# A two-layer graph network on one core: the loads of adj's own columns moved from ScalarE's queue to SyncE's, and the last block's product in three PSUM banks

## The chip, the core and the metric

The kernel runs on one core of a Trainium2 chip, all in float32. The metric is the device time of one launch in microseconds (us). Engines are named as in the profile: PE (TensorE), DVE (VectorE), ACT (ScalarE), POOL (GpSimd) and SP (SyncE). SP computes nothing here; it issues transfers.

## The reference, cut to what matters

`adj` is 3327 x 3327, sparse, with all of the diagonal set and the first nodes' rows and columns by far the fullest. `x` is 3327 x 512. The kernel gets both padded to 3328 rows, 26 blocks of 128, and adj transposed (`adjT`). The hidden width is 128.

```python
h = relu(layernorm(x))
x = x + adj @ (relu(adj @ (h @ W1) + b1) @ W2) + b2        # layer 0

h = relu(layernorm(x))                                     # layer 1
a, b = adj @ h, adj @ h                                    # the same sum twice
attn_a = sigmoid([a, h] @ Wa.T + ba)
attn_b = sigmoid([b, h] @ Wb.T + bb)
hs = h @ W_sa
s_left, s_right = hs @ a_sa[0, :512], hs @ a_sa[0, 512:]
e = where(adj != 0, exp(-leaky_relu(s_left[:, None] + s_right[None, :], 0.01)), 0)
x_a = (e / (e.sum(1) + 1e-5)) @ hs
x_b = adj @ (h @ W_gcnb) + b_gcnb
x = x + sigmoid(attn_a * x_a + attn_b * x_b)
```

## The kernel before, in words

The work has three parts.

**The first pass over adj** (from L593) computes the hidden layer of layer 0 and, at the same time, finds out where adj is not zero. It takes adjT's columns in seven chunks, listed in `back`: six of 512 columns and a last one of 256. I call them passes 0 to 6. In each pass `load_adj` (L295) brings adjT in tiles of two row blocks, 512 KB, through SP's queue, into six buffers (`adjp`). TensorE accumulates `acc_u` over the 26 row blocks j (L622), and DVE reduces each tile to `most`, the largest value of each group of 32 columns (L629). After a pass `make_g` turns its result: `gT`, a relu on ACT (L390), then four transposes into `pg` on PE (L393), a copy on DVE and a store through ACT's queue.

From `most` of one pass, `make_lists` makes, during the next pass, the lists of the groups that are not empty: small steps on PE (`p_off`, `p_sh`, `p_list`, L517 to L567) and on DVE (`at` and others, L482 to L591). By those lists POOL gathers the groups of adj (L180) into the buffers `ae[i]`, one for each block i, which part 3 uses.

Pass 0 has more to do. For each row block j it also loads block j+4 of x (L356, SP's queue, five buffers), normalizes block j+3 on DVE and ACT (`normalize`: `scaled` is its statistics' scale), transposes block j+2 (`pt`, L372) and makes `u` of block j+1 (`pu`, L380). During pass 0 POOL writes constants and clears the 25 buffers `ae[1]` to `ae[25]` one after another (L479). An `ae` buffer must be cleared before anything is loaded into it.

In two kinds of blocks a part of `ae[i]` isn't gathered by a list but loaded at a known place. The 18 blocks in `OWN` get their own columns on the diagonal. The 8 of them in `TOP` also get the columns of the first 64 nodes. This is `load_own` (L210): for each such part and each half of the block's 128 nodes one transfer of 16 KB, 52 in all. They go through ACT's queue. `load_behind` (L335) issues them from pass 2 on at j = 6, 10, 16, 19 and 22, one block each time, and each is tied by `pace` to the `acc_u` matmul of that j. `load_behind` also loads, through ACT's queue, the columns of the first 128 nodes (`a_hub`) in five parts, and pieces of `W_sa` and `W2`. After pass 3 ACT's queue gets `b2_row`.

**The second pass over adj** (L916 to L968) makes layer 0's output, normalizes it and makes layer 1's rows. It reads x again: the first such loads, into buffers called `xb` (L704), are free to go as early as their buffers allow.

**The block loop** (L1278 to L1330) treats the blocks of layer 1: `attend` (scores and exponentials), `sums` (the sums over gathered rows, L1135), `turn` (transposes) and `weigh` (the products with the weights): `p_b` (L1189) and `p_a` (L1197), each in PSUM banks of 128 x 512. `finish` (L1004) joins the two, and per column piece scales `p_a` on ACT, adds on DVE, takes a tanh on ACT, adds x on DVE and stores. For the last block, L1330, the columns go in two pieces, 0 to 257 and 257 to 512 (`WH` is 257), both in one bank; other blocks have one piece.

A scheduler sets the order of the instructions on each engine from the dependencies and the order in the source. `queued(...)` places an instruction behind another one of its own engine's work, `pace` adds a wait. An engine works through its instructions in order, and a queue's waits hold up what stands behind them on the same engine. `psA` and `psB` are two pools of four PSUM banks each.

Of the kernel before, what the change touches and what calls it, by code (L numbers as in the profile page):

```python
# [10 lines left out]
AF = mybir.ActivationFunctionType  # L11
# [7 lines left out]
P = 128  # L19
# [3 lines left out]
HALF = P // 2  # L23
# [32 lines left out]
OWN = TOP + (1, 6, 7, 8, 12, 13, 14, 15, 17, 18)  # L56
# [10 lines left out]
def kernel(  # L67
# [17 lines left out]
    nc = tc.nc  # L85
    NP, D = x.shape
# [4 lines left out]
    back = [(c0, CW) for c0 in range(NP - CW, NP % CW - 1, -CW)]  # L91
# [19 lines left out]
    psA = ctx.enter_context(tc.tile_pool(name="psA", bufs=4, space=bass.MemoryType.PSUM))  # L111
    psB = ctx.enter_context(tc.tile_pool(name="psB", bufs=4, space=bass.MemoryType.PSUM))

    def bank(pool, name):
        return pool.tile([P, CW], F32, tag="bank", name=name)
# [91 lines left out]
                            row_a[:, f : f + 1], NP * NG - 1,  # L207
                        )

    def load_own(i, load):  # L210

        n = segments(i)[0][1]
        for k in range(extra[i]):
            for h in range(2):
                cols = slice(i * P + h * HALF, i * P + (h + 1) * HALF)
                rows = slice(0, HALF) if k else cols
                load(
                    ae[i][h * HALF : (h + 1) * HALF, k : k + n + 1 : n, :GW],
                    adjT[rows, cols].rearrange("j (q i) -> j q i", i=GW),
                )  # L220

    columns = gather_adj()

# [62 lines left out]
    with (  # L286
# [38 lines left out]
        def load_weights(k, load):  # L325
# [2 lines left out]
            elif k == KD:  # L328
                load(W2_sb, W2)

        own_order = iter([
            i for c0, w in back for i in range(c0 // P, (c0 + w) // P) if i in OWN
        ])

        def load_behind(added, n, j):  # L335

            def load(out, in_):
                pace(nc.scalar.dma_start(out, in_), added)

            if j == 3 and n <= HUB_LOADS:  # L340
                load_hub(n - 1, load)
            if j == 13:
                load_weights(n - 1, load)
            if n > 1 and j in (6, 10, 16, 19, 22):
                for i in own_order:
                    load_own(i, load)
                    break

        g = {}

# [252 lines left out]
        for n, c in enumerate(back):  # L603
            c0, w = c
# [44 lines left out]
                    nc.scalar.dma_start(b2_row, b2.partition_broadcast(P))  # L649
            lists = make_lists(n, most)  # L650
            next(lists)
        assert next(own_order, None) is None


        for s in range(2):
# [348 lines left out]
    def finish(pool, i, p_a, p_b, esum, cuts=(0, D)):  # L1004

        x1 = pool.tile([P, D], F32, tag="x1", name=f"x1b_{i}")
        nc.sync.dma_start(x1, x1_dram[i])

        f = pool.tile([P, 3], F32, tag="f", name=f"f_{i}")
        nc.vector.tensor_scalar(f[:, 0:1], esum, SUM_EPS, None, op0=ALU.add)  # L1010
        nc.vector.tensor_tensor(f[:, 1:3], p_b[1][:, WH - 2 : WH], node[i][:, 1:3], ALU.add)
        nc.vector.tensor_scalar(f[:, 1:3], f[:, 1:3], LEAST_LOGIT, None, op0=ALU.max)
        nc.scalar.activation(f[:, 1:3], f[:, 1:3], AF.Exp, scale=-1.0)
        nc.vector.tensor_scalar(f[:, 1:3], f[:, 1:3], 1.0, None, op0=ALU.add)
        r = pool.tile([P, 3], F32, tag="r", name=f"r_{i}")
        nc.vector.reciprocal(r, f)
        nc.vector.tensor_tensor(f[:, 0:1], r[:, 0:1], r[:, 1:2], ALU.mult)
        vb = pool.tile([P, D], F32, tag="vb", name=f"vb_{i}")
        nc.vector.tensor_tensor(vb[:, WH:], p_b[1][:, : D - WH], bg_row[:, WH:], ALU.add)
        read_b = nc.vector.tensor_tensor(vb[:, :WH], p_b[0][:, :WH], bg_row[:, :WH], ALU.add)  # L1020
        va = pool.tile([P, D], F32, tag="va", name=f"va_{i}")
        for c0, c1 in zip(cuts, cuts[1:]):
            a, b = va[:, c0:c1], vb[:, c0:c1]
            read_a = nc.scalar.activation(a, p_a[:, c0:c1], AF.Copy, scale=f[:, 0:1])
            nc.vector.scalar_tensor_tensor(b, b, r[:, 2:3], a, op0=ALU.mult, op1=ALU.add)

            nc.scalar.activation(a, b, AF.Tanh, scale=0.5)
            nc.vector.scalar_tensor_tensor(a, a, 0.5, x1[:, c0:c1], op0=ALU.mult, op1=ALU.add)
            nc.sync.dma_start(out[i * P : (i + 1) * P, c0:c1], a)
        return read_a, read_b  # L1030

    with tc.tile_pool(name="spw", bufs=2) as spw:
# [147 lines left out]
        def weigh(i, tyT, es, cuts=(0, D), sums_first=False, between=None):  # L1180


            p_b = [bank(psB, f"p_b_{i}_{k}") for k in range(2)]
            p_s = p_b[1][:, CW - 1 : CW]
            if sums_first:
                add_up(i, es, p_s)
            for n in (1, 0):
                for k in range(KD):
                    last = nc.tensor.matmul(  # L1189
                        p_b[n][:, :WH], tyT[:, k, 0, :], W_g_sb[:, k, n * WH : (n + 1) * WH],  # L1190
                        start=(k == 0), stop=(k == KD - 1),
                    )
            p_a = bank(psB, f"p_a_{i}")
            with queued(between(last) if between else None):
                for c0, c1 in zip(cuts, cuts[1:]):
                    for k in range(KD):
                        last = nc.tensor.matmul(  # L1197
                            p_a[:, c0:c1], tyT[:, k, 1, :], W_sa_sb[:, k, c0:c1],
                            start=(k == 0), stop=(k == KD - 1),
                        )  # L1200
# [126 lines left out]
            for seg in segs[1:]:  # L1327
                sums(1, seg)
        ty, _ = copy_out(1, taken[1]["acc"], True)
        weigh(1, turn(1, ty, True)[0], taken[1]["es"], (0, WH, D), True)[2]()  # L1330

    over = nc.values_load(overflow[0:1, 0:1], min_val=0, max_val=1)
    with tc.If(over > 0):
# [54 lines left out]
        with (  # L1388
# [25 lines left out]
            for c in range(len(chunks)):  # L1414
# [34 lines left out]
                for b in range(w // P):  # L1449
                    i = c0 // P + b  # L1450
                    cols = slice(b * P, (b + 1) * P)
                    p_s = bank(psB, f"q_s_{i}")
                    nc.tensor.matmul(p_s[:, 0:1], esum[:, cols], ones, start=True, stop=True)
                    p_a = bank(psB, f"q_a_{i}")
                    p_b = [bank(psB, f"q_b_{i}_{k}") for k in range(2)]
                    for t, f0, f1, p in (
                        (yT, None, None, p_a),
                        (tT, 0, WH, p_b[0]),
                        (tT, WH, 2 * WH, p_b[1]),
                    ):  # L1460
                        for k in range(KD):
                            w_sb = W_sa_sb[:, k, :] if f0 is None else W_g_sb[:, k, f0:f1]
                            nc.tensor.matmul(
                                p if f0 is None else p[:, :WH], t[:, k, cols], w_sb,
                                start=(k == 0), stop=(k == KD - 1),
                            )
                    finish(l1w, i, p_a, p_b, p_s[:, 0:1])


# [44 lines left out]
```

## Time and profile before

| | |
|---|---|
| median of 3 runs | 716.57 us (715.82 to 716.97) |
| the profiled execution | 805.4 us |
| its span, first to last instruction | 803.6 us |
| PE busy in the span | 722.7 us, 90% |
| ACT busy | 204.7 us, 25% |
| DVE busy | 485.9 us, 60% |
| POOL busy | 456.3 us, 57% |
| bytes moved | 180.47 MB, mean 225 GB/s |
| end of the passes 0 to 6 (start of the relu `gT`) | 64.98, 89.40, 126.63, 158.59, 185.55, 218.26, 236.36 us |

The profiled execution is 89 us longer than the runs' median, so a duration read from the profile is that of this one execution. Idle time of an engine that isn't the bottleneck costs nothing by itself. In rows of groups, the columns are: line, engine, operation, output and inputs, shapes, count; then busy us and mean ns of one; then idle time before, and what ended most of it. In timelines a row is one instruction or a row of like ones: start, duration, engine, line, operation, count, and in brackets the idle time before it with its releaser. SPq, ACTq are the issuing queues of SP and ACT, in time of the issue and not of the transfer.

### The profile page before, as it was taken

What the parts mean: (1) busy time and instruction counts of PE and PEld (TensorE: products, weight loads), DVE (VectorE), ACT (ScalarE), POOL (GpSimd) and SP (SyncE); (2) the same over time, 40 slices, a digit from 0 to 9 for tenths busy, and PEclk for the clock granted to TensorE, in tenths of its full rate; (3) what the DMA queues carried; (4) which work ended last, traced back from release to release, by engine and by line L of the source; (5) the groups of instructions that cost most, each with busy time, mean ns of one, the idle gap of its engine ahead of it and who ended that gap; (6) DMA issues with size and microseconds to landing.
All of it is one profiled execution on the core that took longest, in us unless ns stands there. A gap on an engine that the chain in (4) does not pass through costs nothing.

```text
span 803.6 us, 11919 instructions
## 1 busy us (share of the span) xinstructions
PE 722.7 (90%) x3715; PEld 392.2 (49%) x3715; DVE 485.9 (60%) x1530; ACT 204.7 (25%) x492; POOL 456.3 (57%) x487
## 2 busy tenths in 40 slices
PE   9999959898789889888896399799999999999994
PEld 7775424343364334444443155345555555555553
DVE  6778949789871326555382177347557456575642
ACT  7870000000000324444270123123123113132311
POOL 2300657566667777667607666776767766675400
PEclk9999979899999999997998799999999899999998
DMA  8789959799869999974258566756666766887410
GB/s 277 250 297 307 300 156 297 235 307 290 253 209 292 360 356 331 334 242 139 66 175 306 149 175 201 226 161 179 212 193 195 206 193 195 246 233 223 136 51 31
DMA packets 105738, 180.47 MB, mean 225 GB/s; under 512 B 21217, under 2 KB 38017, under 8 KB 105666
## 3 DMA queue, kind: packets, MB, share of 16 engines
q1 hardware_dynamic: 63632, 111.91, 41.6%
q0 software_dynamic: 22112, 54.46, 24.2%
q10 hardware_dynamic: 19922, 13.25, 5.3%
q8 instruction: 31, 0.51, 0.3%
q14 instruction: 41, 0.34, 0.1%
HBM read 157.64 MB, written 22.26 MB: 224 GB/s over the span
## 4 chain that ended last, share of the span: by engine, by line
PE 71%; issue 11%; DMA 4%; DVE 4%; POOL 4%; another core or an unknown queue 2%; ACT 2%; SPq 0%; POOLq 0%; ACTq 0%; DVEq 0%
PE acc_u L622 18%; PE acc L1135 10%; PE p_b L1189 9%; PE acc_g L925 9%; PE p_a L1197 8%; PE acc_hub L775 3%; PE pu L380 3%; PE px L723 3%; PE ptt L1149 2%; PE acc_s L882 2%; DMA a<-in_adjT_dram 2%; POOL ae L180 2%; POOL hr L180 1%; PE pt L372 1%
## 5 line engine op out<-in xcount | busy, mean ns | idle before, releaser
L180 POOL DMA_INDIRECT ae<-in_adjT_dram,row_a x178 | 184.0, 1034 | 139.1 <-PE acc_u L622 83.5
L622 PE MATMUL acc_u<-a,rows 128*128 128x512 f32 (+1 forms) x364 | 161.7, 583 | 5.1 <-issue 5.1
L180 POOL DMA_INDIRECT hr<-h_rows,row_h x114 | 120.5, 1057 | 55.5 <-issue 27.4
L1189 PE MATMUL p_b<-W_g_sb,tyT 128*128 128x257 f32 x416 | 103.3, 400 | 9.5 <-issue 8.7
L629 DVE TENSOR_REDUCE most<-a 128x32 f32<-128x1024 f32 (+1 forms) x104 | 103.8, 1009 | 11.6 <-DMA a<-in_adjT_dram 9.0
L180 POOL DMA_INDIRECT rows<-h_rows,row_h x64 | 67.6, 1056 | 58.6 <-DVE es_hub L830 20.8
L1189 PEld LDWEIGHTS p_b<-W_g_sb,tyT 128*128 128x128 f32 x416 | 79.6, 196 | 42.7 <-issue 18.2
L622 PEld LDWEIGHTS acc_u<-a,rows 128*128 128x128 f32 x364 | 67.8, 197 | 64.7 <-issue 61.3
L1197 PE MATMUL p_a<-W_sa_sb,tyT 128*128 128x512 f32 (+2 forms) x216 | 95.6, 583 | 2.9 <-issue 2.4
L180 POOL DMA_INDIRECT g_row<-g_rows,row_h x68 | 71.7, 1055 | 30.1 <-issue 16.0
L925 PE MATMUL acc_g<-a,g 128*128 128x512 f32 (+1 forms) x208 | 84.4, 547 | 2.6 <-issue 2.6
L1164 DVE COPY tyT<-ptt 128x512 f32<-128x512 f32 x51 | 35.0, 686 | 75.7 <-PE ptt L1149 35.6
L1135 PE MATMUL acc<-hr,ae 64*64 64x512 f32 x456 | 59.1, 593 | 2.9 <-issue 2.9
L1197 PEld LDWEIGHTS p_a<-W_sa_sb,tyT 128*128 128x128 f32 x216 | 41.2, 191 | 42.0 <-issue 40.1
L925 PEld LDWEIGHTS acc_g<-a,g 128*128 128x128 f32 x208 | 38.6, 191 | 40.3 <-issue 39.2
L727 DVE SCALAR_TENSOR_TENSOR xb<-px,xb 128x512 f32<-128x512 f32 x26 | 17.9, 689 | 58.0 <-PE px L723 26.1
L390 ACT ACTIVATE gT<-acc_u,b_col 128x512 f32<-128x512 f32 (+1 forms) x7 | 4.6, 657 | 168.7 <-DMA ae<-in_adjT_dram 67.8
L988 DVE SCALAR_TENSOR_TENSOR a_hub<-h_own,w_own 128x512 f32<-128x512 f32 x52 | 35.5, 683 | 9.6 <-DMA rows<-h_rows,row_h 9.5
L1071 ACT COPY s_left<-pl 64x64 f32<-64x64 f32 x42 | 8.7, 207 | 124.0 <-PE pl L1067 71.9
L1135 PEld LDWEIGHTS acc<-hr,ae 64*64 64x64 f32 x456 | 19.9, 133 | 35.3 <-issue 34.1
L268 ACT ACTIVATE rows<-xb,ln_b 128x512 f32<-128x512 f32 x26 | 18.8, 722 | 54.2 <-DVE xb L727 24.7
L1135 PE MATMUL acc<-rows,ae 64*64 64x512 f32 x256 | 32.1, 592 | 0.3 <-issue 0.3
(166 smaller groups left out, 979.5 us busy)
## 6 DMA issues: line engine op xcount, KB each, us to landing
a<-in_adjT_dram SPq DMA_DIRECT2D x129, 512.0 KB
h_rows<-rows SPq DMA_DIRECT2D x26, 260.0 KB
h_own<-h_rows SPq DMA_DIRECT2D x26, 260.0 KB
x<-in_x_dram SPq DMA_DIRECT2D x26, 256.0 KB
xb<-in_x_dram SPq DMA_DIRECT2D x26, 256.0 KB
x<-xb ACTq DMA_DIRECT2D x26, 256.0 KB
x1b<-x SPq DMA_DIRECT2D x26, 256.0 KB
out_dram<-va SPq DMA_DIRECT2D x25, 256.0 KB
```

The source lines that it names most:

```text
L180: return nc.gpsimd.indirect_dma_start(out=dst, out_offset=None, in_=table, in_offset=bass.IndirectOffsetOnAxis(ap=rows, axis=0), bounds_ch ...
L380: nc.tensor.matmul(pu[:, :HID], hT[:, k, :], W1_sb[:, k, :], start=(k == 0), stop=(k == KD - 1))
L622: added = nc.tensor.matmul(acc[:, :w], u[j], a[:, :w], start=(j == 0), stop=(j == NB - 1))
L629: nc.vector.tensor_reduce(most[:, : w // GW, j : j + both], tiles.rearrange("p k (b i) -> p b k i", i=GW), axis=AX.X, op=ALU.max, apply_ab ...
L723: on_pe[0] = last_row[2] = nc.tensor.matmul(px, sTs.pop(i), W2_sb, start=True, stop=True)
L775: return nc.tensor.matmul(acc_hub[k], s, made_row(i)[:, :D], start=(n == 0), stop=(n == NB - 1))
L925: on_pe[0] = nc.tensor.matmul(acc[:, :w], g[j], a[:, n % per, :], start=(n == 0), stop=(n == NB - 1))
L988: nc.vector.scalar_tensor_tensor(junk, h[:, :D], 1.0, w_own[:, s, :], op0=ALU.mult, op1=ALU.mult, accum_out=node[i][:, 1 + s : 2 + s],)
L1135: added = nc.tensor.matmul(taken[i]["acc"][h][q * HALF : (q + 1) * HALF, :], both[half_p, q * n + k, :], taken[i][k0][k][half_p, q, :D], s ...
L1164: last = nc.vector.tensor_copy(dst, src)
L1189: last = nc.tensor.matmul(p_b[n][:, :WH], tyT[:, k, 0, :], W_g_sb[:, k, n * WH : (n + 1) * WH], start=(k == 0), stop=(k == KD - 1),)
L1197: last = nc.tensor.matmul(p_a[:, c0:c1], tyT[:, k, 1, :], W_sa_sb[:, k, c0:c1], start=(k == 0), stop=(k == KD - 1),)
```

## The change

`load_own` becomes a generator that issues one of its transfers at each step, on SP's queue. `own_loads` strings the generators of the 18 blocks together. `load_behind` takes one step at each odd j of every pass after the first, whatever is left is issued after the last pass, and the loads are no longer tied to a matmul. In `weigh` the product `p_a` becomes a list of banks, one for each column piece, and `finish` reads each piece from its own bank. The last block has three pieces: 0 to 257, 257 to 448 and 448 to 512 (`HALF` is 64). For all other blocks it stays one piece in one bank of `psB`.

```diff
-    def load_own(i, load):
+    def load_own(i):
 
         n = segments(i)[0][1]
         for k in range(extra[i]):
             for h in range(2):
                 cols = slice(i * P + h * HALF, i * P + (h + 1) * HALF)
-                rows = slice(0, HALF) if k else cols
-                load(
+                rows = slice((k - 1) * HALF, k * HALF) if k else cols
+                nc.sync.dma_start(
                     ae[i][h * HALF : (h + 1) * HALF, k : k + n + 1 : n, :GW],
                     adjT[rows, cols].rearrange("j (q i) -> j q i", i=GW),
                 )
+                yield
...
-        own_order = iter([
-            i for c0, w in back for i in range(c0 // P, (c0 + w) // P) if i in OWN
-        ])
+        own_loads = iter(
+            None
+            for c0, w in back
+            for i in range(c0 // P, (c0 + w) // P)
+            if i in OWN
+            for _ in load_own(i)
+        )
...
             if j == 13:
                 load_weights(n - 1, load)
-            if n > 1 and j in (6, 10, 16, 19, 22):
-                for i in own_order:
-                    load_own(i, load)
-                    break
+            if j % 2:
+                next(own_loads, None)
...
-        assert next(own_order, None) is None
+        for _ in own_loads:
+            pass
...
-        for c0, c1 in zip(cuts, cuts[1:]):
+        for p, c0, c1 in zip(p_a, cuts, cuts[1:]):
             a, b = va[:, c0:c1], vb[:, c0:c1]
-            read_a = nc.scalar.activation(a, p_a[:, c0:c1], AF.Copy, scale=f[:, 0:1])
+            read_a = nc.scalar.activation(a, p[:, : c1 - c0], AF.Copy, scale=f[:, 0:1])
...
-            p_a = bank(psB, f"p_a_{i}")
+            p_a = [bank(psA if n else psB, f"p_a_{i}_{n}") for n in range(len(cuts) - 1)]
             with queued(between(last) if between else None):
-                for c0, c1 in zip(cuts, cuts[1:]):
+                for p, c0, c1 in zip(p_a, cuts, cuts[1:]):
                     for k in range(KD):
                         last = nc.tensor.matmul(
-                            p_a[:, c0:c1], tyT[:, k, 1, :], W_sa_sb[:, k, c0:c1],
+                            p[:, : c1 - c0], tyT[:, k, 1, :], W_sa_sb[:, k, c0:c1],
...
-        weigh(1, turn(1, ty, True)[0], taken[1]["es"], (0, WH, D), True)[2]()
+        weigh(1, turn(1, ty, True)[0], taken[1]["es"], (0, WH, D - HALF, D), True)[2]()
```

More of the change, by code (lines that the diff above doesn't have):

```diff
@@ L1466 @@
                             )
-                    finish(l1w, i, p_a, p_b, p_s[:, 0:1])
+                    finish(l1w, i, [p_a], p_b, p_s[:, 0:1])
 def kernel(**inputs):
```

## The prediction

> **What bounds the kernel now.** I read the page's totals and its chain of waits first, then the groups that the edit touches, then the first pass over adj cut at the seven `gT` activations (one ends each pass), then the timelines of SP, POOL, ACT and PE at the places the edit moves things.
>
> ```profile
> PE 722.7 (90%) x3715; PEld 392.2 (49%) x3715; DVE 485.9 (60%) x1530; ACT 204.7 (25%) x492; POOL 456.3 (57%) x487
> PE 71%; issue 11%; DMA 4%; DVE 4%; POOL 4%; another core or an unknown queue 2%; ACT 2%; SPq 0%; POOLq 0%; ACTq 0%; DVEq 0%
> L622 PE MATMUL acc_u<-a,rows 128*128 128x512 f32 (+1 forms) x364 | 161.7, 583 | 5.1 <-issue 5.1
> L390 ACT ACTIVATE gT<-acc_u,b_col 128x512 f32<-128x512 f32 (+1 forms) x7 | 4.6, 657 | 168.7 <-DMA ae<-in_adjT_dram 67.8
> ```
>
> TensorE carries the chain (71%), the first pass's `acc_u` most of all. DMA is 4% of the chain, SP's and ACT's queues 0%: to the sum, loads are hidden, so a change of who issues them acts only where one holds back PE. The last row shows such a place: before `gT`, which PE's next transposes need, ACT is mostly busy with `ae` loads. The passes, from the busy time in windows (columns: PE, PEld, DVE, ACT, POOL, clock, DMA share, GB/s):
>
> ```profile
> 16.00:40.50 24.50, 24.50 (x158) 18.54 (x157) 19.91 (x66) 19.76 (x45) 11.79 (x57) 1.00 0.78 254
> 64.98:89.40 24.42, 24.42 (x104) 11.01 (x103) 21.62 (x48) 0.69 (x1) 4.07 (x4) 1.00 0.93 303
> 158.59:185.55 26.96, 26.15 (x109) 11.63 (x107) 23.77 (x53) 0.69 (x2) 18.42 (x19) 1.00 0.98 310
> 185.55:218.26 32.71, 25.98 (x141) 12.23 (x141) 30.28 (x69) 0.69 (x1) 21.66 (x21) 1.00 0.89 273
> ```
>
> In pass 0 (the first 24.5 us of it) and pass 1 PE has no gap. Pass 1, 24.42 us, is the length of a pass that nothing holds up. Pass 4 is longer, with DMA at 0.98, and pass 5 longer still. So what costs in pass 0 is paid in full, and what frees pass 4 or 5 is gained.
>
> **The change, part by part.** The sum stands against the profiled execution, 805.4 us (span 803.6, 1.8 around it). The runs' median is 716.57: 88.8 below, about the chain's 11% of "issue" (88 us). I take the edit's differences over unscaled. A measurement of this kernel tells 0.2%, 1.43 us, from no change: faster is below 715.1, slower above 718.0.
>
> *1. What moves.* 52 loads of 16 KB leave ACT's queue, 18 blocks in passes 2 to 5, and go to SP's. The source spreads them over passes 1 to 4 (odd j, 13 a pass). They are no longer tied to a matmul, though, and the compiled order of the changed kernel shows where the scheduler puts them: 22 of 52 in pass 0, between x loads and tiles, the rest in passes 1 to 3, about one a tile, the last ahead of pass 4's second tile. On ACT one costs 0.6 to 0.7 us of issue; on SP an x load 0.33, a tile 0.43, so 0.6 is my value there too (0.33 to 0.7). Their data is small: the 7168 packets of 128 B take 13 ns each, eight an engine, 0.1 us a load. The order moves a second thing: SP's five loads of `xb` (256 KB each, 54 to 60 us, end of pass 0) go into pass 4 and the start of pass 5.
>
> *2. Pass 0: a cost.* The first own load in SP's order is of block 3 and the next of block 24; each waits until POOL has cleared that `ae` buffer, and x loads and tiles stand behind it in SP's order.
>
> ```profile
> 16.80 2.41 SPq L356 DMA_DIRECT2D x<-in_x_dram  x2
> 19.26 0.43 SPq L301 DMA_DIRECT2D a<-in_adjT_dram  x1
> 21.07 2.52 SPq L356 DMA_DIRECT2D x<-in_x_dram  x2
> 23.64 0.43 SPq L301 DMA_DIRECT2D a<-in_adjT_dram  x1
> ```
>
> ```profile
> 21.00 2.24 POOL L479 MEMSET ae<- 128x448 f32 x6
> 23.29 4.49 POOL L479 MEMSET ae<- 128x320 f32 x18
> ```
>
> ae3 is clear at 21.9, ae24 at 27.6. After x_11 (16.80) SP sits until 21.9, issues three pieces, and x_12 goes at 23.9 in place of 18.9, tile 8 at 24.3 in place of 19.3. Then it sits until 27.6: x_14 at 29.6 in place of 23.3, tile 10 at 30.0 in place of 23.6. Landings: x 2.5 us after issue, a tile 3.8 (27.43 less 23.64). Tile 8 is there at 28.2 for its matmul at 28.45, x_12 at 26.4; tile 10 at 33.8 for 32.83, x_14 at 32.1, where before its statistics ran on DVE at 27.2. DVE takes work in order, so block 13's later steps come behind that wait: its transposes start near 34.65 in place of 33.69 (+0.96), block 14's 0.2 later still. From there the pieces fit in the 2.19 us that PE takes per row block. PE has no gap to absorb it: +1.1 us. Ends: 0 (PE's transposes of a later block taken ahead, POOL earlier in an unprofiled run) and +3.3 (the first rival's working, below).
>
> *3. Pass 4: `xb` arrives, own loads leave.* Sixteen own loads leave (1.7 us of DMA), 1.31 MB comes in (3.4 us at 390 GB/s, the most that a 2 us window moved), in a pass with the DMA share at 0.98. The `b2_row` load ends on DVE's path (1.96 us of waiting at 163.3), and behind it DVE's list steps feed PE's `p_list` with no slack (its matmuls come at the rate DVE makes `at`). One `xb` in front is 0.65 us: +0.5 us. Ends 0 (the tiles have six buffers) and +2.
>
> *4. ACT's queue free for `gT`: a gain.*
>
> ```profile
> 176.84 8.61 ACTq L338 DMA_DIRECT2D ae<-in_adjT_dram  x8
> 185.55 0.69 ACT L390 ACTIVATE gT<-acc_u,b_col 128x512 f32<-128x512 f32 x1 [26.27 <-DMA a<-in_adjT_dram]
> ```
>
> ```profile
> 186.29 0.66 PE L393 MATMUL pg<-ident,gT 128*128 128x128 f32 x4 [0.90 <-issue]
> ```
>
> Pass 4's accumulation ends at 184.5, ACT's eighth load only at 185.45, the activation starts 0.1 later, and PE stands 0.90 us ahead of `pg`. The wait's label (a tile) isn't its cause: the tile had landed. It goes whole: -0.9 us. In passes 2 and 3 ACT's loads end before the accumulation does (125.45 for 126.63, 157.28 for 158.59), but PE stalls 10 and 4 us there on "issue", much of which an unprofiled run may not have; then these wait too. Ends 0 and -2.7.
>
> **A rule against the change.** On ACT the row is that 8.61 us of eight issues in front of `gT`. The Trainium skill ("DMA: Bandwidth & Descriptors", Issuing engines are not separate DMA queues) says all DMAs share the same 16 engines whoever starts them, and spreading issues saves only the sequencer's time, usually small. By the rule alone this part is worth 0 to ACT and adds 52 x 0.6 us to the queue that feeds PE. By the row, ACT's sequencer time is what PE waited for, 0.90 us. But the same page (Anatomy of one DMA — SWDGE (gpsimd) path) says that a semaphore wait sits on the issuing sequencer, and this is step 2's mechanism. The rule makes the sum of 2 and 4 +1.1, the rows +0.2. I keep the rows.
>
> *5. SP's lateness: a gain.* In pass 1, with no own loads yet, SP issues each tile 0.03 us after its buffer is free. From pass 2 on, tiles go 1 to 5 us late (5.07 for pass 2's row block 10, 1.65 to 2.56 in pass 5), because the eight completion semaphores of the hardware queues go round and a tile then waits for an ACT load that is tied to a matmul. PE uses a tile about 9 us after issue, which covers nearly all. Where it doesn't, in pass 5, DVE waits 0.54 us for a tile at 190.9 and PE then waits 1.78 us for DVE's `at`. I take -0.5 (0 to -1.5).
>
> *6. The tail.*
>
> ```profile
> 790.95 3.61 PE L1197 MATMUL p_a<-W_sa_sb,tyT 128*128 128x257 f32 x16
> 794.60 0.84 ACT L1024 ACTIVATE va<-p_a,f 128x257 f32<-128x257 f32 x2 [4.32 <-PE p_a L1197]
> ```
>
> All sixteen `p_a` matmuls are done before ACT reads the first piece: one bank, one wait. With a bank each, the first read starts near 792.8. The second half, 255 wide, becomes 191 and 64: PE ends 0.4 to 0.65 later (eight more records, small ones), but what follows is 64 columns wide, and ACT's order read, tanh, read, read, tanh, tanh ends near 796.3, where the last DVE step now ends at 796.9. One more output load, 0.4 of issue, comes earlier than the last one. -0.5 us. Ends -0.9 and +0.2. If the wait for the whole bank were kept, it would be +0.4.
>
> *Sum:* +1.1 +0.5 -0.9 -0.5 -0.5 = -0.3 us: 805.1 for the profiled execution, 716.3 for the median. Nothing else on PE, POOL or DVE changes but a few places of `junk_w`, which fill DVE gaps at no cost; without the gap one is 0.7 us of DVE, in step 3's range.
>
> **The rivals.** *Slower: SP stands at POOL's clears (step 2's place) for longer than the lead covers.* DVE's statistics of block 14 start at 32.1 in place of 27.2, 4.9 late, and its in-order queue may hand all of that on to the blocks behind. What PE has in hand is the lead of `h` over its transposes: block 13's activation ends near 32.1, its transposes start at 33.69, 1.6. Then pass 0 pays 4.9 - 1.6 = 3.3, and with my other terms (-1.4) the sum is +1.9, 718.5. It decides from 2.8 on, where the sum passes the 1.43 that can be told. For it: 24.5 us with no PE gap, and DVE's fixed order. Against: only two places wait, and six tile buffers.
>
> *Faster: the unprofiled passes 2 and 3 have the `gT` wait too.* Step 4 becomes -2.7, step 5 -1.0, pass 0 +0.8, pass 4 0, tail -0.5: -3.4, 713.2. For it: 88.8 us of profile are missing from the median, and PE's "issue" stalls lie just there. Against: in the trace the wait is in one pass only.
>
> *It doesn't do what it says:* the loads are not between adj's tiles evenly, 22 crowd into pass 0, where ACT's queue never was in the way, and the transfers were hidden before. Then the tail alone is left: 716.1.
>
> **How the numbers follow.** The forecast 0.40 (716.3, itself 714.6 to 718.3), slower 0.30 (717.6 to 720.5), faster 0.25 (712.2 to 715.1), tail alone 0.05. Of the forecast's 0.40, 0.06 falls below 715.1 and 0.05 above 718.0; of the slower rival 0.03 within the bound, of the faster 0.01, of the last 0.02 below. Faster 0.06 + 0.24 + 0.02 = 0.32; same 0.29 + 0.03 + 0.01 + 0.03 = 0.36; slower 0.05 + 0.27 = 0.32. The range, 712.8 to 720.0, leaves out the outer tenth on either side.
>
> **What would show it.** Step 2: SP's first own load at 21.9 and next block's at 27.6, a PE gap near 33.7, pass 0 longer by 1.1 (0: refuted; 3.3: the slower rival). Step 4: pass 4's `gT` right at the accumulation's end, `pg` with no wait. Step 5: tiles issued as their buffers come free. Step 3: `b2_row`'s wait on DVE over 1.96. Step 6: the first read near 792.8 with 1.8 us less wait, counted from the last block's first `p_a`. A gain or loss in the second pass over adj or in the block loop, where nothing is edited but the end, would make the whole account wrong.

## The result, and the profile after

The changed kernel took 714.7 us against 716.75 for before (medians of 20 runs each): 0.9977 of it, 95% interval 0.9955 to 0.9999. A second comparison gave 715.95 against 717.77, 0.9963 (0.9943 to 0.9982). So it is faster: by 1.6 and 2.7 us by these ratios, by 2.05 and 1.82 us by the medians. (The ratios, here and below, are of fast runs alone, those within 1.5% of the kernel's fastest; where every kernel took about 790 us this leaves out up to 7 of 22 runs, and the ratio there is not that of the medians.) The page of its profile, in lines that answer to those shown of before:

```profile
span 714.1 us, 11911 instructions
PE 694.5 (97%) x3723; PEld 383.7 (54%) x3723; DVE 483.4 (68%) x1532; ACT 203.0 (28%) x494; POOL 461.6 (65%) x487
PE 83%; DMA 7%; DVE 6%; ACT 1%; POOL 1%; issue 1%; SPq 0%; ACTq 0%; POOLq 0%; DVEq 0%
L625 PE MATMUL acc_u<-a,rows 128*128 128x512 f32 (+1 forms) x364 | 158.0, 575 | 2.0 <-DMA a<-in_adjT_dram 1.5
L393 ACT ACTIVATE gT<-acc_u,b_col 128x512 f32<-128x512 f32 (+1 forms) x7 | 4.6, 657 | 142.2 <-PE acc_u L625 117.2
```

The span is 89.5 us shorter than in the first profile of before, and that isn't the change: "issue", 11% of the chain there, is 1% here. The last row is the change: what ACT waits for ahead of `gT` is now mostly PE's accumulation (117.2 of 142.2 us) and no longer a load. To compare stage by stage, a profile of before without the issue stalls was needed. The second profile of before (first experiment) is one: span 713.6 us. Its passes 2 to 5, from the busy time in windows (PE, PEld, DVE, ACT, POOL, clock, DMA share, GB/s):

```profile
89.45:116.55 27.10, 25.51 (x105) 10.93 (x103) 23.29 (x52) 0.69 (x2) 20.46 (x22) 1.00 0.92 290
116.55:142.66 26.11, 24.76 (x107) 11.18 (x107) 26.11 (x57) 0.69 (x2) 20.32 (x20) 1.00 1.01 326
142.66:169.24 26.58, 25.64 (x107) 11.71 (x107) 24.10 (x57) 0.69 (x2) 20.49 (x21) 1.00 0.97 306
169.24:198.91 29.67, 26.91 (x139) 12.50 (x140) 28.46 (x67) 0.68 (x2) 21.47 (x22) 0.94 0.95 290
```

The same passes of the changed kernel:

```profile
91.98:116.40 24.42, 24.42 (x104) 11.01 (x103) 23.24 (x53) 0.69 (x1) 18.72 (x19) 1.00 1.02 335
116.40:140.94 24.54, 24.54 (x108) 11.07 (x107) 24.54 (x56) 0.69 (x1) 19.03 (x19) 1.00 0.99 322
140.94:166.59 25.65, 25.60 (x108) 11.67 (x107) 24.99 (x58) 0.69 (x2) 19.59 (x20) 1.00 1.03 358
166.59:197.57 30.98, 29.00 (x141) 13.22 (x140) 28.19 (x64) 0.68 (x1) 23.96 (x24) 0.89 0.86 274
```

In passes 2 to 4, PE now has no gap: span and PE busy time agree within 0.05 us, where before they stood 1.59, 1.35 and 0.94 apart. The three passes are 5.2 us shorter. They also vary by themselves: in a third profile with before's loads (the three banks alone, below) they take 26.61, 24.54 and 27.49, and against that one they are 4.0 us shorter. Pass 5 is longer in the changed kernel at a lower clock, 0.89 against 0.94. In its second profile it is pass 4 that has the lower clock (27.95 us at 0.94), and pass 5 takes 26.50 at 1.00. The clock's dips move from profile to profile, so a stage is compared only at equal clock.

What passes 2 to 4 lost, seen on PE's timeline in the second profile of before:

```profile
111.43 4.56 PE L622 MATMUL acc_u<-a,rows 128*128 128x512 f32 x10 [1.03 <-DMA a<-in_adjT_dram]
117.29 0.66 PE L393 MATMUL pg<-ident,gT 128*128 128x128 f32 x4 [1.30 <-ACT gT L390]
143.40 0.66 PE L393 MATMUL pg<-ident,gT 128*128 128x128 f32 x4 [1.34 <-ACT gT L390]
169.97 0.66 PE L393 MATMUL pg<-ident,gT 128*128 128x128 f32 x4 [0.89 <-ACT gT L390]
```

Here the label names the cause: `pg` waits for `gT`, three times, 3.53 us in sum. ACT's timeline shows why `gT` is late in the first of them: eight own loads are issued until 116.50, and `gT` follows at 116.55, though the accumulation had ended at 115.13.

```profile
106.14 10.36 ACTq L338 DMA_DIRECT2D ae<-in_adjT_dram  x8
116.55 0.69 ACT L390 ACTIVATE gT<-acc_u,b_col 128x512 f32<-128x512 f32 x1 [26.41 <-DMA ae<-in_adjT_dram]
```

The 10.36 us are not all issue. The eight issues take 0.60 to 0.67 us each, 5.04 in sum; the other 5.3 us ACT stands between them, at the semaphores of matmuls and of earlier transfers. In passes 3 and 4 it is 4.95 of 9.04 and 4.88 of 8.59.

The cost is in pass 0, which now ends at 67.56 (67.75 in the second profile) in place of 65.03. SP's timeline of the changed kernel:

```profile
17.14 0.33 SPq L359 DMA_DIRECT2D x<-in_x_dram  x1
22.27 2.05 SPq L217 DMA_DIRECT2D ae<-in_adjT_dram  x3
24.43 0.53 SPq L359 DMA_DIRECT2D x<-in_x_dram  x1
25.01 0.43 SPq L302 DMA_DIRECT2D a<-in_adjT_dram  x1
25.54 0.41 SPq L359 DMA_DIRECT2D x<-in_x_dram  x1
27.96 1.91 SPq L217 DMA_DIRECT2D ae<-in_adjT_dram  x3
29.97 0.54 SPq L359 DMA_DIRECT2D x<-in_x_dram  x1
30.55 0.43 SPq L302 DMA_DIRECT2D a<-in_adjT_dram  x1
```

SP stands from 17.47 to 22.27 and from 25.95 to 27.96, ahead of the first pieces of block 3 and of block 24. PE pays at two tiles (first the two matmuls in the first profile of before, then after):

```profile
28.45 1.02 PE L622 MATMUL acc_u<-a,rows 128*128 128x512 f32 x2
32.83 1.02 PE L622 MATMUL acc_u<-a,rows 128*128 128x512 f32 x2
```

```profile
29.12 1.10 PE L625 MATMUL acc_u<-a,rows 128*128 128x512 f32 x2 [0.50 <-ACT ln_a L255]
35.31 1.10 PE L625 MATMUL acc_u<-a,rows 128*128 128x512 f32 x2 [1.54 <-DMA a<-in_adjT_dram]
```

The first comes 0.67 us late and the second 2.48, so another 1.81. Both are the first use of a tile that left SP late. The first one's label, an ACT step, isn't where the time went: `acc_u` reads only `u` and the tile, and ACT's last copy for that `u` had ended at 26.73.

The end, second profile of before and then after (the last block's `p_a`, ACT's first read of it, the output's issues):

```profile
701.04 3.62 PE L1197 MATMUL p_a<-W_sa_sb,tyT 128*128 128x257 f32 x16
704.70 0.84 ACT L1024 ACTIVATE va<-p_a,f 128x257 f32<-128x257 f32 x2 [4.32 <-PE p_a L1197]
706.64 0.81 SPq L1029 DMA_DIRECT2D out_dram<-va  x2
```

```profile
703.21 4.03 PE L1201 MATMUL p_a<-W_sa_sb,tyT 128*128 128x257 f32 x24
705.14 0.48 ACT L1028 ACTIVATE va<-p_a,f 128x257 f32<-128x257 f32 x1 [2.60 <-PE p_a L1201]
707.09 1.98 SPq L1033 DMA_DIRECT2D out_dram<-va  x3
```

ACT reads the first piece 1.93 us after the first `p_a` instead of 3.66. PE needs 0.41 longer for the smaller pieces, and from the first `p_a` to the last issue's end it is 5.86 us instead of 6.41. The span's end doesn't show this gain by itself: from the first `p_a` to it are 12.5 us in before's second profile, 12.7 with the three banks alone, 10.9 and 11.5 in the two profiles of the changed kernel, so what follows the last issue varies by more.

Between the first pass and the tail nothing is edited, but the profiles differ. The second pass takes 134.20 us in before's second profile, 136.22 with the three banks alone, 135.07 and 135.24 in the changed kernel. The block loop, in the second profile of before and then after:

```profile
375.35:701.04 325.69, 320.01 (x1874) 181.61 (x1873) 205.49 (x726) 81.89 (x201) 223.63 (x212) 1.00 0.70 209
374.80:703.21 328.41, 323.40 (x1874) 183.15 (x1873) 205.52 (x726) 81.89 (x201) 226.14 (x213) 0.99 0.70 208
```

It is 2.7 us longer, all of it PE's busy time (3.4 us more) at a lower clock. In the second profile of the changed kernel it is 5.1 us longer (330.80), 3.2 of it busy time; the other 1.9 are not explained. So the two profiled executions end level, with spans of 713.6 and 714.1 us: PE is idle 4.6 us less in the changed kernel (19.6 against 24.2) and busy 5.1 longer, at mean clocks of 0.987 and 0.995. The profiles show where the kernel gains and loses; that it is faster as a whole, the timed runs alone show.

### The profile page after: what moved, and what is told of

The parts are those of the page before. It is cut to its first block, busy times and chain, and to the rows that moved or that the text cites. A ratio compares the mean times of both kernels' runs of the same rounds, so it can differ in the third digit from the quotient of the medians.

```text
span 714.1 us, 11911 instructions
## 1 busy us (share of the span) xinstructions
PE 694.5 (97%) x3723; PEld 383.7 (54%) x3723; DVE 483.4 (68%) x1532; ACT 203.0 (28%) x494; POOL 461.6 (65%) x487
## 4 chain that ended last, share of the span: by engine, by line
PE 83%; DMA 7%; DVE 6%; ACT 1%; POOL 1%; issue 1%; SPq 0%; ACTq 0%; POOLq 0%; DVEq 0%
PE acc_u L625 16%; PE acc L1139 15%; PE p_b L1193 14%; PE p_a L1201 13%; PE acc_g L929 8%; PE acc_hub L779 4%; PE ptt L1153 3%; DMA a<-in_adjT_dram 3%; PE px L727 3%; DVE most L632 2%; PE pu L383 2%; PE acc_s L886 1%; PE pt L375 1%; PE p_list L570 1%; DMA b_row<-in_b_dram 1%
## 5 line engine op out<-in xcount | busy, mean ns | idle before, releaser
L180 POOL DMA_INDIRECT ae<-in_adjT_dram,row_a x178 | 187.8, 1055 | 113.3 <-PE acc_u L625 67.6
L625 PE MATMUL acc_u<-a,rows 128*128 128x512 f32 (+1 forms) x364 | 158.0, 575 | 2.0 <-DMA a<-in_adjT_dram 1.5
L1193 PE MATMUL p_b<-W_g_sb,tyT 128*128 128x257 f32 x416 | 98.8, 390 | 2.3 <-DVE tyT L1168 1.9
L1193 PEld LDWEIGHTS p_b<-W_g_sb,tyT 128*128 128x128 f32 x416 | 77.7, 192 | 32.7 <-DVE ae L1114 5.7
L1201 PE MATMUL p_a<-W_sa_sb,tyT 128*128 128x512 f32 (+3 forms) x224 | 93.9, 563 | 0.0
L929 PEld LDWEIGHTS acc_g<-a,g 128*128 128x128 f32 x208 | 38.5, 190 | 38.4 <-issue 33.3
L1139 PE MATMUL acc<-hr,ae 64*64 64x512 f32 x456 | 54.2, 600 | 0.0
L393 ACT ACTIVATE gT<-acc_u,b_col 128x512 f32<-128x512 f32 (+1 forms) x7 | 4.6, 657 | 142.2 <-PE acc_u L625 117.2
L731 DVE SCALAR_TENSOR_TENSOR xb<-px,xb 128x512 f32<-128x512 f32 x26 | 17.9, 688 | 34.0 <-PE px L727 33.8
L1153 PEld LDWEIGHTS ptt<-ident,ty 128*128 128x128 f32 x208 | 24.3, 141 | 14.3 <-issue 13.5
L1139 PE MATMUL acc<-rows,ae 64*64 64x512 f32 x256 | 30.2, 591 | 0.0
```

Source lines behind the costliest of these rows:

```text
L180: return nc.gpsimd.indirect_dma_start(out=dst, out_offset=None, in_=table, in_offset=bass.IndirectOffsetOnAxis(ap=rows, axis=0), bounds_ch ...
L625: added = nc.tensor.matmul(acc[:, :w], u[j], a[:, :w], start=(j == 0), stop=(j == NB - 1))
L929: on_pe[0] = nc.tensor.matmul(acc[:, :w], g[j], a[:, n % per, :], start=(n == 0), stop=(n == NB - 1))
L1139: added = nc.tensor.matmul(taken[i]["acc"][h][q * HALF : (q + 1) * HALF, :], both[half_p, q * n + k, :], taken[i][k0][k][half_p, q, :D], s ...
L1153: moved = nc.tensor.transpose(pt[:, k * P : (k + 1) * P], ty[h][:, k * P : (k + 1) * P], ident)
L1193: last = nc.tensor.matmul(p_b[n][:, :WH], tyT[:, k, 0, :], W_g_sb[:, k, n * WH : (n + 1) * WH], start=(k == 0), stop=(k == KD - 1),)
```

## The experiments

My theory after the result: the move costs pass 0 some 2.5 us because SP stands at POOL's clearing, and gives back more in passes 2 to 4, where `gT` had stood behind ACT's loads. The rivals: all of the gain is the tail; or the queue doesn't matter, only where in a pass ACT has its loads.

On some chips every kernel took about 790 us, with PE standing on "issue" as in the first profile of before; the ratios there are to before on the same chip, and of those profiles only pass 0, which is free of such stalls, is read.

**The kernel before, again.** No edit.

> The kernel before once more, for a profile without the 88 us of issue stalls that its first profile had. Theory: against the changed kernel, pass 0 is 2.6 us shorter (65.0), passes 1 to 3 take 24.4 to 24.6 us as there, passes 4 and 5 together are 2 to 4 us longer (a gT activation held by ACT's loads, a tile or list step that comes late), and from the last block's first p_a to the last output's issue it takes 6.4 us against 5.9. Rival (the move of the loads gains nothing in the passes, all is in the tail): passes 2 to 5 as long as in the changed kernel within 0.5 us, and the changed kernel's gain must then come from elsewhere than the passes.

This is one execution, of 715.34 us; the 51 runs of before beside it have a median of 717.04. Passes 0 to 6 end at 65.03, 89.45, 116.55, 142.66, 169.24, 198.91 and 213.84. Pass 0 and the tail are as expected. Passes 4 and 5 together are 0.4 us shorter than in the changed kernel, not 2 to 4 longer, with pass 5's clock at 0.94 against 0.89. The gain is earlier, in passes 2 and 3 (2.7 and 1.6 us) and in pass 4 (0.9). The end of pass 4 sums up what the move gives and costs until then: 169.24 here and 168.23 with the three banks alone, against 166.59, 166.30 (own loads alone) and 169.08 (the one with pass 4 at 0.94) with the loads moved.

**Own loads on SP alone.** The changed kernel with `p_a` as before:

```diff
-            p_a = [bank(psA if n else psB, f"p_a_{i}_{n}") for n in range(len(cuts) - 1)]
+            p_a = bank(psB, f"p_a_{i}")
...
-        weigh(1, turn(1, ty, True)[0], taken[1]["es"], (0, WH, D - HALF, D), True)[2]()
+        weigh(1, turn(1, ty, True)[0], taken[1]["es"], (0, WH, D), True)[2]()
```

> Only the own columns' loads on SP's queue, p_a as before. Theory (the move costs pass 0 2.6 us and gives back somewhat more in passes 3 to 5): about 1.0 us faster than before, 0.9985; pass 0 ends at 67.5. Rival (all of the gain is the tail, the move costs what pass 0 shows): 0.5 to 2.5 us slower, up to 1.0035.

716.03 against 717.04: 0.9987 (0.9966 to 1.0009). The middle is where the theory put it, but the interval takes in no change. The profile is the changed kernel's, pass by pass: pass 0 ends at 67.31, passes 2 to 4 take 24.42, 24.54 and 25.61.

**The three banks alone.** The kernel before with the edit of `weigh` and `finish`, none in `load_own`.

> Only p_a's three banks, loads as before. Theory: 0.5 to 0.7 us faster than before, 0.999, which a timing of this kernel hardly tells from none; in the profile the last output is issued 5.9 us after the last block's first p_a instead of 6.4. Rival (all of the gain is the tail): 1.7 us faster or more, 0.9977. Passes as in the kernel before.

717.12 against 717.04: 1.0011 (0.9984 to 1.0037). By timing it can't be told from before, but it speaks against a gain of 1.7 us or more by the tail, which would be 0.9977, just outside the interval. In its profile the last output is issued 5.86 us after the first `p_a`, to the hundredth as in the changed kernel, so the tail's gain up to the last issue is 0.55 us. Its loads are before's, and `pg` waits for `gT` 1.79 us in pass 2 and 1.41 in pass 4, but not in pass 3: 3.2 us in sum.

**Every own load pinned behind a tile, none in pass 0.**

```diff
             if j % 2:
-                next(own_loads, None)
+                with queued(tile_loads[-1]):
+                    next(own_loads, None)
```

(`tile_loads` holds the tile loads as they are issued.)

> The changed kernel with each own load placed behind the tile load of its row block (queued behind it on SP), so that none is in pass 0, 13 in each of passes 1 to 4. Theory (pass 0 pays 2.6 us because x loads and tiles stand behind own loads that wait for POOL's clearing): pass 0 ends at 65.0 again, the whole is 2.6 us faster than the changed kernel and 4 us faster than before, 0.994. Rival (the x loads' delay is not what pass 0 waits for, or the saved time is given back in pass 4 where 13 loads now are): same as the changed kernel, 0.9975 to 0.999.

718.42 against 717.04: 1.0025 (1.0002 to 1.0048). Slower, and neither theory had it so. Pass 0 ends at 65.25, as the theory said, but passes 2, 3 and 4 take 25.30, 27.03 and 30.32 (the last at a clock of 0.94). PE waits for tiles there, and SP's timeline has a reason:

```profile
118.86 0.38 SPq L304 DMA_DIRECT2D a<-in_adjT_dram  x1
125.63 0.60 SPq L217 DMA_DIRECT2D ae<-in_adjT_dram  x1
126.34 0.53 SPq L304 DMA_DIRECT2D a<-in_adjT_dram  x1
```

```profile
130.67 1.98 PE L628 MATMUL acc_u<-a,rows 128*128 128x512 f32 x4 [0.88 <-DMA a<-in_adjT_dram]
153.45 2.97 PE L628 MATMUL acc_u<-a,rows 128*128 128x512 f32 x4 [0.51 <-DMA a<-in_adjT_dram]
```

The next tile's buffer was free at 118.95, but ahead of that tile SP has an own load that it doesn't issue until 125.63. The semaphore numbers in the trace say what this load waits for. The transfers of SP and ACT signal their completion through eight semaphores that they share (numbers 100, 102 and 104 to 109), and a transfer waits for the earlier one that has its number. This own load has 102, which ACT's store of g, issued at 119.56, had before it (and the next own load has 105, after ACT's `a_hub` load, issued at 120.02). With an own load behind every tile, the eight numbers come round after about four tiles.

A measure for this is how late SP issues a tile of passes 2 to 5 after its buffer is free (the end of the last matmul or reduce of the tile six ahead), summed over the 52 tiles, worked out from the traces: 61.6 us in before (51.4 in the three-banks profile, which has the same loads), 14.3 in the changed kernel, 134.1 here. The kernel with more of it than before is slower than before, the one with less is faster; that goes together, and isn't shown to be the whole cause.

**Own loads left on ACT, earlier in the pass.**

```diff
-            if n > 1 and j in (6, 10, 16, 19, 22):
+            if n > 1 and j in (5, 8, 11, 15, 18):
```

> The kernel before with its own loads still on ACT's queue and tied to matmuls, but at j = 5, 8, 11, 15, 18 instead of 6, 10, 16, 19, 22, so that ACT is through with them when a pass ends. Theory (PE waits for gT behind ACT's loads in passes 2, 3 and 4, 1.3, 1.3 and 0.9 us in the second profile of before): these three waits go, pass 0 stays at 65.0, and the whole is 3.5 us faster than before, 0.995, so about 2 us faster than the changed kernel. Rival (the passes are held by SP's lateness, which stays while tiles wait for ACT's paced loads): passes 2 to 4 within 1 us of before in sum, 0.999 to 1.000.

791.87 against 792.33: 1.0016 (0.9981 to 1.005), on a chip with the issue stalls. The gain of 0.995 is outside the interval. Since the stalls could hide it, the edit was run again with the three banks:

> The kernel before with own loads left on ACT's queue at j = 5, 8, 11, 15, 18, and the last block's p_a in three banks. Theory (the gain of the move is that gT no longer stands behind ACT's loads; the queue as such doesn't matter): pass 0 ends at 65.1, gT starts right at the end of the accumulation in passes 2 to 4, 3.5 us shorter in sum than before, the tail 0.5 shorter: 0.9945 of before. Rival (tiles on SP still wait for ACT's paced loads, and that was part of the gain): passes 2 to 5 keep 1 us or more of waits for tiles or for DVE's list steps, 0.997 to 0.999.

720.72 against 717.77: 1.0041 (1.0019 to 1.0064), slower than before. The theory's part came as it said: `gT` starts at the end of the accumulation, and no `pg` waits. But tiles and DVE's list steps are waited for in its place:

```profile
114.98 1.12 PE L622 MATMUL acc_u<-a,rows 128*128 128x512 f32 x2 [0.41 <-DMA a<-in_adjT_dram]
147.95 5.42 PE L622 MATMUL acc_u<-a,rows 128*128 128x512 f32 x12 [0.55 <-DMA a<-in_adjT_dram]
175.90 0.35 PE L529 MATMUL p_sh<-after,shift 128*128 128x416 bf16 x1 [1.00 <-DVE after L511]
181.50 0.20 PE L567 MATMUL p_list<-step,at 128*64 128x27 bf16 x1 [2.68 <-DVE at L556]
```

SP's lateness over passes 2 to 5 is 82.7 us, more than in before. So issuing ACT's loads earlier doesn't do what moving them to SP does: while they are tied to matmuls and share the semaphores, tiles wait for them, in these two places in the pass more at the earlier one. The gain of the move is two things, the freed `gT` and the freed tiles. The move also undid the tie to the matmuls, and no run left the loads on ACT without it, so how much is the queue's and how much the tie's is open.

**Own loads in pass 0 behind the clearing.** 30 loads pinned behind the x loads from the 15th on, 13 in pass 1, 9 in pass 2:

```diff
+        PLACES = {15: 2, 16: 2, 17: 3, 18: 2, 19: 3, 20: 2, 21: 3, 22: 2, 23: 3, 24: 2, 25: 6}
...
                         load_x(j + 4)
+                        with queued(x_loaded[j + 4]):
+                            for _ in range(PLACES.get(j + 4, 0)):
+                                next(own_loads)
```

> The changed kernel with own loads pinned on SP: 30 in pass 0, two or three behind each x load from the 15th on (all behind POOL's clearing), 13 in pass 1 and 9 in pass 2, one behind each tile. Theory (pass 0 pays only for the two waits on POOL's clearing): pass 0 ends at 65.0 to 65.3, passes 1 to 4 as in the changed kernel but for up to 0.9 in pass 2, where one load behind each tile made tiles late in the run with all of them pinned; the whole 1.5 to 2.5 us faster than the changed kernel, 0.994 to 0.9955 of before. Rival (SP's issue time for own loads in pass 0 makes x late by itself): pass 0 ends at 67 or later, the whole as the changed kernel.

794.24 against 792.33: 1.0011 (0.9983 to 1.0039). Pass 0 ends at 68.39, as the rival said. PE's timeline:

```profile
56.53 1.10 PE L632 MATMUL acc_u<-a,rows 128*128 128x512 f32 x2 [1.05 <-ACT h L261]
66.40 2.81 PE L632 MATMUL acc_u<-a,rows 128*128 128x512 f32 x6 [1.31 <-DMA a<-in_adjT_dram]
```

SP shows the second one's source: six pieces behind the last x load, and three tiles that go only after them.

```profile
53.20 3.86 SPq L217 DMA_DIRECT2D ae<-in_adjT_dram  x6
57.16 2.45 SPq L304 DMA_DIRECT2D a<-in_adjT_dram  x3
```

So a piece's 0.65 us of SP isn't free where SP is full. With 30 pieces in the second half of pass 0 they cost 3.4 us (68.39 against 65.03), with no wait for the clearing at all.

**The clearing at the very start.** POOL clears the `ae` buffers before pass 0's constants, with pass 0's own loads pinned at the changed kernel's places (three behind x_11 and so on) and the rest one behind a tile, as in the pinned run:

```diff
+        for t in ae[1:]:
+            nc.gpsimd.memset(t[:, :, :GW], 0.0)
...
-            for t in ae[1:]:
-                nc.gpsimd.memset(t[:, :, :GW], 0.0)
```

> The changed kernel with the ae buffers cleared by POOL at the very start, and the own loads of pass 0 pinned at the same places as in the changed kernel (three behind x_11, three behind x_13 and so on), the others one behind each tile in passes 1 to 3. Read for pass 0 alone: theory (the wait for the clearing is the cause) it ends at 65.0 to 65.3; rival (the issue time, three times 0.65 us in front of an x load and a tile) it ends at 66 to 67.6. As a whole: 1 us faster to 2 us slower than the changed kernel, since passes 2 and 3 have the loads behind each tile.

791.44 against 792.33: 0.9943 (0.9915 to 0.9971). Read for pass 0: it ends at 65.40, so the wait is the cause, and the issue of these pieces without it, 22 in the pass, costs 0.4 us at most.

**The changed kernel's own order, without the wait.** The same clearing, with all 52 own loads pinned at the places where the changed kernel's SP has one. SP's order of transfers is the same, in all 350 of both traces; only which block's piece goes first differs.

> The changed kernel with the ae buffers cleared by POOL at the very start, and every own load pinned at the place on SP where the changed kernel has one (the order of SP's transfers is the same, only no own load waits for a clearing). Theory (the two waits for the clearing are what pass 0 pays): pass 0 ends at 65.1 to 65.4, passes 1 to 6 as in the changed kernel, the whole 2.2 us faster than it, about 0.9945 of before. Rival (what pass 0 saves is lost again, to a lower granted clock or in pass 4 and 5): the same as the changed kernel within 0.7 us.

712.68, against 715.95 for the changed kernel and 717.77 for before in the same comparison: 0.9942 of before (0.9923 to 0.9961). SP no longer stands between x_11 and the pieces, and the tile leaves at 20.37 in place of 25.01:

```profile
16.90 0.33 SPq L372 DMA_DIRECT2D x<-in_x_dram  x1
17.32 2.37 SPq L217 DMA_DIRECT2D ae<-in_adjT_dram  x3
19.79 0.53 SPq L372 DMA_DIRECT2D x<-in_x_dram  x1
20.37 0.43 SPq L304 DMA_DIRECT2D a<-in_adjT_dram  x1
```

Pass 0 ends at 64.98, passes 2 and 3 take 24.42 and 24.54, and SP's lateness is 13.6 us. This version is faster than before, and faster than the changed kernel too: the two intervals against before overlap a little, but the means of 22 runs each are 712.99 and 715.73, 2.7 us apart, with a standard error of 0.7. The changed kernel beside it:

> The changed kernel once more, on the same chip as the two runs below. Expected as in its first measurement: 0.9977 of before (0.9955 to 0.9999), pass 0 ending at 67.5, PE nearly without a gap in passes 1 to 4 unless the chip shows the issue stalls again that the first profile of before had.

It is the second comparison given at the top: 0.9963, pass 0 ending at 67.75.

**The first loads of `xb` back to the end of pass 0.** cleared_order, with five `load_next()` calls pinned behind the tiles (2304, 4), (2304, 6) and (2304, 8), and beside it cleared_order again:

> As cleared_order (the clearing at the start, own loads at the changed kernel's places), and the first five loads of xb moved from pass 4 to the turn from pass 0 to pass 1, where the kernel before has them. Theory of step 3 of the prediction (in pass 4 they cost some tenths of a us by a late b2_row or late tiles): pass 4 takes 25.3 to 25.4 us at full clock instead of 25.65 to 25.9, its first 36 p_list records take 1.5 us instead of 1.84, pass 1 stays at 24.42; the whole 0.2 to 0.5 us faster than cleared_order. Rival (they cost nothing in pass 4, or as much in pass 1): pass 4 as in cleared_order, or pass 1 longer by 0.3 or more, the whole the same.

> The kernel of cleared_order again, beside xb_early on the same chip and for its interval: 0.994 of before (0.992 to 0.996), pass 0 ending at 65.0, passes 2 and 3 at 24.4 and 24.5.

788.0 and 791.12 against 793.34: 0.9915 (0.9885 to 0.9945) and 0.9966 (0.9941 to 0.9991). Both are faster than before; that xb_early is the better of the two is likely by the middles, but the intervals overlap. Pass 4 could not be read at full clock and without issue stalls in these profiles, so what `xb` costs there isn't settled by this pair.

## Why the prediction was right, point by point

The range held both results, and no change (0.36) and faster (0.32) were nearly level. The sum of -0.3 us stands against about -2. That the range held is in part luck: it was 7 us wide and centred on no change, and two mistakes of size lay on opposite sides, the cost in pass 0 put 1.4 us too low and the gain at `gT` 2.3 to 2.6 too low.

*Step 1, what moves.* In the trace 30 of the 52 loads, not 22, are issued before pass 0 ends: 19 among its x loads, the others between tiles that SP issues ahead. The first of the five `xb` loads goes at the end of pass 3 (137.9), the other four in pass 4.

*Step 2, pass 0: mechanism right, size wrong.* SP stood where it was said, at 22.27 and 27.96 (21.9 and 27.6 were written), and cleared_same and cleared_order show that this wait is the cause. The term was +1.1 and is +2.5 to +2.7. The mis-sized term is the tiles' landing: I gave a tile 3.8 us from issue to its matmul, found tile 8 in time and tile 10 0.97 late (33.8 for 32.83), about what DVE's statistics gave (+0.96). But tile 8, issued at 25.01 and not at 24.3, was 0.67 late already, and tile 10, issued at 30.55 and not at 30.0, was used at 35.31, 4.76 us after. So its 1.5 us beyond the 33.8 are 0.55 of later issue and 0.96 of longer landing. The tiles decided, and no wait for DVE's later steps is seen at PE. The cost came close to the slower rival's threshold of 2.8.

*Step 4, `gT`: the mechanism right, the faster rival's size.* -0.9 was taken, because the trace of before showed the wait in one pass. Without the issue stalls it is there in passes 2, 3 and 4: 3.5 us, beyond even the -2.7 of the rival (3.2 in passes 2 and 4 with the three banks alone). The mistake is one of reading: in passes 2 and 3 of the first profile PE stood 10 and 4 us on "issue", so ACT had time to finish, and "no delay seen" was taken for "no delay", though the rival had said so and was given 0.25. The 88.8 us missing from the runs were also not all "issue": of the 90.0 us between the two profiles of before, 33.3 are PE's busy time (722.7 against 689.4) at a clock of 0.959 and not 0.995, and 56.7 are idle time.

*Step 5, SP's lateness: right in kind, wrong in place.* The wait for DVE's `at` in pass 5 is still there (1.72 us in before's second profile, 1.70 after), so nothing was gained where I put the -0.5. In the changed kernel's second profile it is only 0.24, behind a pass 4 at a clock of 0.94; in cleared_order, with both passes at 1.00, it is 1.74. So this wait depends on the pass before, and equal clock in pass 5 alone doesn't make two of them comparable. A tile wait of 1.03 us in pass 2 went, and act_early_banks and pinned have more lateness and are slower; it is larger than the half microsecond that I gave it. ("1 to 5 us late from pass 2 on" was read too widely: 32 of the 52 tiles there went within 0.2 us, and the 5.07 is row block 20's.)

*Step 3, `xb` and `b2_row`: not seen.* The rows of pass 4's first 36 `p_list` records, in the second profile of before and in after:

```profile
153.65 1.87 PE L567 MATMUL p_list<-step,at 128*64 128x27 bf16 x36
```

```profile
151.94 1.84 PE L570 MATMUL p_list<-step,at 128*64 128x27 bf16 x36
```

They are as long, and DVE's wait for `b2_row` is 0.60 us after and 1.71 before. The +0.5 was 0 within what these two profiles show; in the second profile of the changed kernel the row takes 2.45 us and in cleared_order 2.12, with the three banks alone 2.26, so it varies without the move. (The most that a window of 2 us moved is 398 GB/s and not 390, which changes nothing in the term.)

*Step 6, the tail:* -0.5 written, -0.55 measured, up to the last issue.

*The sum by what was measured:* +2.5 - 3.5 - 1.0 - 0.55 = -2.55 us, near the second comparison's -2.7 and within the first one's interval (-3.2 to -0.1), but beyond the -1.8 and -2.05 of the medians. It takes the stages where the wait is seen and leaves out pass 5, the second pass and the block loop, where single profiles differ by as much. A loss in the block loop was to make the whole account wrong; the profiles have one of 2.7 and 5.1 us, most of it busy time at a lower clock, and whether the edit has a part in it is open.

*The rule.* By it (the Trainium skill, "DMA: Bandwidth & Descriptors", Issuing engines are not separate DMA queues) the move was worth nothing on ACT and a cost on SP. With the measured terms it would make the sum of steps 2 and 4 +2.5, the rows -1.0, and the kernel got faster. The issuing engine's time isn't small where its next instruction is what PE waits for (3.5 us), but only about half of that time was issue (5.04 of 10.36 us), the rest waits between the issues. The same page's other sentence (Anatomy of one DMA — SWDGE (gpsimd) path), that a semaphore wait sits on the issuing sequencer, fits both: ACT's waits ahead of `gT`, and SP's 4.80 us ahead of block 3's pieces.

How much of these results the clock makes: within the 59 runs of before of the second comparison, a line fitted to time against granted clock falls by 6 us for each 0.01. Read off such lines, one for each kernel, at a clock of 0.992, before is 716.6, the changed kernel 716.1, cleared_order 713.2 and act_early_banks 718.3, each to about 0.3 us (act_early_banks 0.5). The order is the same, but of the changed kernel's second gain only 0.5 us is left. Its first 20 runs give 714.9; the runs of before measured with them have no clock on record, those beside only_own give 716.3. Whether the edit brings the higher clock or it is chance isn't shown.

## What to carry to other kernels

A load moved to another engine's queue takes its waits along: look for what the receiving queue would stand at, and take that wait away first (here POOL's clearing at the start, 3.3 us by the medians, 1.5 by the ratios). Where transfers share a few semaphores, as these do eight, small loads scattered one by one between large ones can tie the large ones together; the lateness of issue after a buffer is free shows it (134.1 us against 14.3 here). And a wait that a stalled profile doesn't show may still be in the runs: if the profile is 12% longer than the runs, read the stage's slack without the stall.

## What the runs showed of the hardware

- The same program took about 716 us on some chips and 790 on others. Between the two profiles of before, 56.7 of the 90.0 us are PE standing idle, much of it on "issue" (rows of 0.5 to 2 us ahead of single matmuls, most of all among `p_list` and `acc_u` in pass 2), and 33.3 are PE being busy longer at a mean clock of 0.959 and not 0.995. The cause of both is open.
- In the profiles of about 715 us the granted clock of pass 4 or pass 5 fell to between 0.89 and 0.94 in most, and for one and the same kernel in pass 5 of one profile and in pass 4 of the next. PE's gaps in passes 2 and 3 don't explain it: with gaps there, pass 5 was at 0.94 in before and at 1.00 with the three banks alone; with none, at 0.89 in the changed kernel and at 1.00 in cleared_order.
